# A new order for the first chunk of an encoder: transposes, roundings and loads of one graph kernel

## The chip, the cores and the metric

The kernel runs on one core of a Trainium2 chip. The metric is the time of one execution in microseconds of device time. The median of 3 runs of the kernel before is 487.85 us (485.99 to 488.41).

## The reference

Two graph layers stand one after the other, each on a layer norm with a relu and each with a residual. There are 1250 nodes with 1024 features, 20000 edges, and an inner width of 500. Cut to what matters:

```python
h = jnp.maximum(_layernorm(x), 0.0)
# first layer
e   = sigmoid(h @ wenc.T + benc)              # the encoder: 1250 x 1024 by 1024 x 500
agg = segment_sum((e @ conv_weight)[src] * edge_weight[:, None], dst)
x   = x + (agg + e @ lin_weight.T) @ wdec.T + bdec
# second layer
h   = jnp.maximum(_layernorm(x), 0.0)
x   = x + normalised_adjacency(src, dst) @ (h @ W.T + b)
```

The change touches only the start of the program: the layer norm and the encoder product of the first 250 nodes.

## The kernel before, in words

The nodes lie in 10 tiles of 125 rows, and two tiles make a chunk of 250 nodes; the encoder goes over five chunks. Every float32 product is computed in three parts from values that are split into a rounded high part and the low rest: high by high, high by low, low by high. So each operand needs a rounding ("high", a copy into the rounded type) and a difference ("low") before TensorE can use it.

For a tile `t` of the input the steps are:

- `load_x(t)`: a transfer of 512 KB from DRAM, issued by SyncE. Tiles 0 and 1 are loaded in two pieces of half rows.
- `stats t` (`row_stats`, L310 and L312): mean and variance on VectorE, in two halves of the row (`stats 1 0` is the first half alone) and an aggregate; then `factors` (L297 to L301), three small steps on GpSimd that turn them into scale and bias.
- `norm t` (`normed`, L273): the norm and relu in place on ScalarE, for the whole row or a half.
- `half t q` (`half_transposed`, L282 to L285): TensorE transposes four blocks of 128 columns into one PSUM buffer; a copy on ScalarE rounds them into `hnh` (L284; `halfv` has VectorE do it); VectorE writes the difference into `hnl` (L285).

The encoder's weights come in four transfers `wencf0` to `wencf3` of 500 KB. `high j` rounds one of them on ScalarE (L324, 128x1000), `highv j` on VectorE; `low k` writes the low part of half of one on VectorE (L330, 128x500), `lowp k` on GpSimd.

Chunk 0's product (L579) runs `k` over the eight blocks of 128 features. It keeps four PSUM accumulators, one for each 125 of the 500 outputs. For `k` = 0 the eight products that need only `hnh` come first, then the four that need `hnl`; `k` = 1 to 5 take twelve products each; the last two blocks go output by output, each followed by the sigmoid (L559). Chunk 1 and later chunks use the same products in another line (L347).

The order of all this is written out by hand: the table `ORDER` says which steps are recorded ahead of chunk 0's first product (slot `(0, -1)`) and after each block (`(0, 0)` after `k` = 0, and so on), and the recording order is the order of instructions on every engine until the encoder ends. Later stages are ordered by a scheduler. SyncE issues the loads in the order x0, x0, x1, x1, wencf0, wencf1, x2, wencf2, x3, wencf3, x4; from the ninth transfer on, an issue waits until the transfer eight places ahead of it has landed. Memory places come from a fixed plan. 18 products on zeroes (`warm`, L247) keep TensorE busy from the start until the first tile is there.

Of the kernel before, what the change touches and what calls it, by code (L numbers as in the profile page):

```python
# [41 lines left out]


ORDER = {
    (0, -1): "stats 0, stats 1 0, stats 1 1, norm 0 0, halfv 0 0, norm 0 1, high 0, low 0, lowp 1, "
             "highv 1, lowp 3, norm 1 0, norm 1 1, half 1 0, lowp 2, stats 2 0, stats 2 1, half 0 1, "
             "high 2, half 1 1, lowp 4",
    (0, 0): "stats 3 0, stats 3 1, lowp 5, stats 4, norm 2, high 3",
    (0, 3): "half 2 0, norm 3",
    (0, 4): "half 2 1",  # L50
    (0, 5): "low 7, lowp 6, stats 5, half 3 1, half 3 0",
    (0, 6): "norm 4",
    (0, 9): "stats 6",
    (1, 0): "norm 5",
    (1, 2): "half 5 0, stats 7, half 4 1",
# [81 lines left out]
def kernel(  # L137
# [16 lines left out]
    nc = tc.nc  # L154
# [3 lines left out]
    T = 125  # L158
# [22 lines left out]
    ps_t = ctx.enter_context(tc.tile_pool(name="ps_t", bufs=2, space=bass.MemoryType.PSUM))  # L181
    ps_oh = ctx.enter_context(tc.tile_pool(name="ps_oh", bufs=2, space=bass.MemoryType.PSUM))
# [9 lines left out]
    def move(dst_, src_, rest=nc.sync):  # L192

        n = dst_.shape[0]
        m = n - n % 16
        nc.sync.dma_start(dst_[:m], src_[:m])
        if m < n:
            rest.dma_start(dst_[m:], src_[m:])
# [6 lines left out]
    def rows(a, t):  # L205

        return a[: min(P, N - t * T)]

    def load_x(t):
        xs[t] = arena.tile([P, D], F32, f"x{t}")  # L210
        pieces = 2 if t < 2 else 1
        for i in range(pieces):
            cs = slice(i * D // pieces, (i + 1) * D // pieces)
            move(rows(xs[t], t)[:, cs], rows(x[t * T :, :], t)[:, cs])

    in_order = ExitStack()
    in_order.enter_context(tc.manual_schedule())
    load_x(0)
    load_x(1)
    wencf = [arena.tile([P, 2, EMB], F32, f"wencf{j}") for j in range(KD // 2)]  # L220
    for j, f in enumerate(wencf):
        nc.sync.dma_start(f, wenc_v[:, 2 * j : 2 * j + 2, :])
        if j > 0:
            load_x(j + 1)
    benc_sb = const.tile([T, EC], F32, name="benc_sb")
    nc.sync.dma_start(benc_sb, benc)
    dsb = const.tile([T, NS // T, GRAN], I32, name="dsb")
# [44 lines left out]
    def relu(to, xt, rs):  # L272
        nc.scalar.activation(to, xt, AF.Relu, bias=rs[:, 1:2], scale=rs[:, 0:1])  # L273

    def half_transposed(t, q, pool=ps_t, tag="pt", copy=nc.scalar.copy):

        hi, lo = hn[t // 2]
        at = slice(t % 2 * T, (t % 2 + 1) * T)
        p = pool.tile([P, 512], F32, tag=tag, name="pt")[:, : 4 * T].rearrange("p (k n) -> p k n", k=4)
        for k in range(4):  # L280
            kk = 4 * q + k
            nc.tensor.transpose(p[:, k, :], xs[t][:T, kk * P : (kk + 1) * P], ident[:T, :T])  # L282
        ks = slice(4 * q, 4 * q + 4)
        copy(hi[:, ks, at], p)  # L284
        nc.vector.tensor_sub(lo[:, ks, at], p, hi[:, ks, at])  # L285

    hn = {}

# [34 lines left out]
    def high_wenc(j, copy=nc.scalar.copy):  # L323
        copy(wenc[j][:, 0], wencf[j])  # L324
# [53 lines left out]
    def edge_rows():  # L378
        c = edges["below"]
        half = c.shape[1] // 2  # L380
        ps = ps_t.tile([P, 512], F32, tag="pt", name="pstart")
        for b in range(NB):
            for j in range(half):
                nc.tensor.matmul(
                    ps[:T, b : b + 1], c[:, j, b * T : (b + 1) * T], ones_b[:T],
                    start=(j == 0), stop=(j == half - 1),
                )
        arena.give("cmp0", "cmp1")
        sf = const.tile([T, NB], F32, name="sf")
        row = const.tile([T, NB], I32, name="row")  # L390
        nc.vector.tensor_scalar(sf, ps[:T, :NB], -1.0, 0.0, op0=OP.add, op1=OP.max)
        nc.vector.tensor_scalar(row, sf, float(NW - 1), None, op0=OP.min)
        edges["row"] = row
# [316 lines left out]
    parts = {}  # L710
    halves = []

    def half(t, q, copy=nc.scalar.copy):
        half_transposed(t, q, *((ps_oh, "poh") if t == 1 else (ps_t, "pt")), copy)
        halves.append(t)
        if halves.count(t) == 2:
            arena.give(f"x{t}")

    def split_lin():
        parts["lin"] = split_square("lin")  # L720

    what = {
        "stats": row_stats, "norm": normed, "half": half, "halfv": lambda t, q: half(t, q, nc.vector.tensor_copy), "load": load_x,
        "high": high_wenc, "highv": lambda j: high_wenc(j, nc.vector.tensor_copy),
        "low": low_wenc, "lowp": lambda k: low_wenc(k, nc.gpsimd),
        "starts": edge_starts, "rows": edge_rows, "gather": edge_gather, "fields": edge_fields,
# [107 lines left out]
    at = 0  # L834
# [17 lines left out]
    def decode(t, half):  # L852
        c, i = divmod(t, 2)
        ns = slice(i * T, (i + 1) * T)
        cs = slice(half * HALF, (half + 1) * HALF)
        p = ps_acc.tile([P, 512], F32, tag="acc", name="pdec")
        terms = []
        for k in range(EC):
            r = T + (k == 0)
            terms.append(  # L860
                (
                    [aggT[c][:r, s, k, ns] for s in range(2)],
                    [wdec[k][:r, s, cs] for s in range(2)],
                )
            )
        product(p[:T, :], terms)
        return p
# [220 lines left out]
    for i, t in enumerate(tiles):  # L1088
        st = small.tile([T, 2, 6], F32, name="st")
        for half in range(2):  # L1090
            slot = 2 * i + half
            p = decode(t, half)
# [541 lines left out]
```

## Time and profile before

| | |
|---|---|
| median of 3 runs | 487.85 us |
| the profiled execution | 487.37 us |
| its span, first to last instruction | 485.6 us |
| mean granted TensorE clock | 0.993 |
| TensorE busy | 474.9 us, 98% |
| VectorE, ScalarE, GpSimd busy | 336.0, 174.3, 81.5 us |
| first product of chunk 0 | 12.70 us |
| first product of chunk 1 | 26.58 us |

A profile is one execution. Its page gives the busy time of each engine, the span in 40 slices of 12.1 us, the transfers and the costliest groups; the timeline lists instructions in order of their start, with the idle time of the engine ahead of them and what ended it. PE is TensorE's matmul, PEld its weight load, DVE VectorE, ACT ScalarE, POOL GpSimd and SP SyncE. Times in the timeline are from the start of the span.

### The profile page before, as it was taken

Reading aid. Unit: us, or ns where it says so; the run is one execution under the profiler, and the core shown is the slowest. Engines: PE = TensorE matmul, PEld = TensorE weight load, DVE = VectorE, ACT = ScalarE, POOL = GpSimd, SP = SyncE. Lnnn points to the kernel's source line nnn. Section 1 sums busy time; section 2 is a strip of 40 time slices with the busy share of each in tenths; the row PEclk is TensorE's granted clock in tenths of the full one; section 3 lists DMA queues with packets and bytes.
Section 4 is the critical chain, followed back from the end, with each engine's and each line's share of the span. In section 5 each row is a group of like instructions: output and inputs, shape, how many; then the busy total and the mean of one; then the engine's idle time right before and its main releaser. Section 6 shows DMA issues by size and latency. Waiting matters only on the chain. (4 is left out here: it accounts for less than half of the span.)

```text
span 485.6 us, 9225 instructions
## 1 busy us (share of the span) xinstructions
PE 474.9 (98%) x3614; PEld 431.2 (89%) x3614; DVE 336.0 (69%) x763; ACT 174.3 (36%) x453; POOL 81.5 (17%) x134
## 2 busy tenths in 40 slices
PE   6999999999999999999999999999999999999995
PEld 3999999998889999999878889999998887788784
DVE  6777479977697958884457776968798554555541
ACT  4585543553433243451253345323265021110000
POOL 4734252410000010161123641000000000000000
PEclk9899999999999999999999999999999999999998
DMA  8993103000000204401999621022429064445441
GB/s 284 368 272 85 32 2 84 1 29 28 29 29 28 70 4 135 164 1 29 205 253 262 200 86 45 2 82 92 163 79 236 11 165 112 112 122 128 124 97 49
DMA packets 50899, 52.20 MB, mean 108 GB/s; under 512 B 29728, under 2 KB 39592, under 8 KB 50847
## 3 DMA queue, kind: packets, MB, share of 16 engines
q1 hardware_dynamic: 50449, 51.09, 37.2%
q8 instruction: 30, 0.49, 0.4%
q0 software_dynamic: 320, 0.39, 0.3%
q14 instruction: 22, 0.18, 0.1%
q10 hardware_dynamic: 78, 0.05, 0.0%
HBM read 34.61 MB, written 17.45 MB: 107 GB/s over the span
## 5 line engine op out<-in xcount | busy, mean ns | idle before, releaser
L1175 PE MATMUL pout<-w,zs 128*125 128x512 f32 (+1 forms) x336 | 100.8, 383 | 0.0
L347 PE MATMUL pagg<-A,h 125*125 125x250 f32 x600 | 74.7, 282 | 0.0
L1175 PEld LDWEIGHTS pout<-w,zs 128*125 128x125 f32 x336 | 61.3, 186 | 14.1
L347 PEld LDWEIGHTS pagg<-A,h 125*125 125x125 f32 x600 | 71.4, 187 | 0.1
L347 PE MATMUL pdec<-wdec,agg 126*125 126x512 f32 x240 | 56.2, 395 | 0.0
L347 PEld LDWEIGHTS pdec<-wdec,agg 126*125 126x125 f32 x240 | 44.7, 187 | 11.1
L1183 DVE SCALAR_TENSOR_TENSOR res<-pout,dinv,res 125x512 f32<-125x512 f32 (+1 forms) x21 | 15.2, 725 | 49.5 <-PE pout L1175 49.5
L952 PE MATMUL pz<-cts,y 125*128 125x312 f32 (+1 forms) x320 | 47.3, 307 | 0.2 <-DVE cts L818 0.2
L952 PEld LDWEIGHTS pz<-cts,y 125*128 125x128 f32 x320 | 46.4, 189 | 0.5 <-DVE cts L818 0.5
L523 ACT CAST A<-poh 125x100 fp32r<-125x100 f32 x150 | 25.5, 258 | 49.3 <-PE poh L513 49.3
L534 DVE TENSOR_TENSOR A<-poh,A 125x100 fp32r<-125x100 f32 x150 | 26.9, 234 | 13.3 <-ACT cnt L529 12.8
L952 PE MATMUL pz<-ct,y 125*128 125x312 f32 (+1 forms) x240 | 35.7, 307 | 0.0
L952 PEld LDWEIGHTS pz<-ct,y 125*128 125x128 f32 x240 | 35.0, 189 | 0.1
L347 PE MATMUL penc<-hnh,wenc 128*125 128x250 f32 x256 | 34.3, 283 | 0.0
L482 DVE TENSOR_TENSOR oh<-cols,eb 128x640 bf16<-128x640 bf16 x50 | 25.9, 522 | 8.5 <-PE poh L513 6.2
L347 PEld LDWEIGHTS penc<-hnh,wenc 128*125 128x125 f32 x256 | 31.3, 187 | 0.0
L347 PE MATMUL plin<-hT,lin 125*125 125x250 f32 x240 | 30.1, 282 | 0.0
L347 PEld LDWEIGHTS plin<-hT,lin 125*125 125x125 f32 x240 | 28.6, 187 | 0.0
L347 PE MATMUL pconv<-conv,hT 125*125 125x500 f32 x120 | 28.6, 392 | 0.0
L508 PE MATMUL poh<-oh 128*128 128x100 bf16 x250 | 28.1, 206 | 0.0
L512 PE MATMUL poh<-oh 128*128 128x50 bf16 x250 | 27.1, 187 | 0.0
L513 PE MATMUL poh<-oh 128*128 128x50 bf16 x250 | 27.0, 184 | 0.0
(180 smaller groups left out, 843.4 us busy)
## 6 DMA issues: line engine op xcount, KB each, us to landing
x<-in_x_dram SPq DMA_DIRECT2D x14, 512.0 KB
x_d<-x SPq DMA_DIRECT2D x9, 512.0 KB
res<-x_d SPq DMA_DIRECT2D x9, 512.0 KB
out_dram<-res SPq DMA_DIRECT2D x19, 224.0 KB
c_d<-cnt SPq DMA_DIRECT2D x10, 320.0 KB
cr<-c_d SPq DMA_DIRECT2D x10, 312.5 KB
x<-in_x_dram SPq DMA_DIRECT2D x8, 256.0 KB
wencf<-in_wencT_dram SPq DMA_DIRECT2D x4, 500.0 KB
```

The costliest lines, as they stand in the source:

```text
L347: nc.tensor.matmul(p, left[i], right[j], start=(part == 0 and n == 0), stop=(part == 2 and n == len(terms) - 1),)
L482: nc.vector.tensor_tensor(pairs(bo), pairs(cols).unsqueeze(1).to_broadcast([P, PB, P // 2, 2]), eb[:, gs].unsqueeze(2).to_broadcast([P, PB ...
L508: nc.tensor.matmul(p[:, g, :], left, mv[:, g, 0:2, :].rearrange("p q m -> p (q m)"), start=True, stop=False,)
L512: nc.tensor.matmul(p[:, g, M:], left, mv[:, g, 2, :], start=False, stop=False)
L513: nc.tensor.matmul(p[:, g, M:], left, mv[:, g, 3, :], start=False, stop=True)
L523: nc.scalar.copy(hi, whole)
L534: nc.vector.tensor_sub(lo, whole, hi)
L952: nc.tensor.matmul(p, left[m, which][:, s, j, :], right[:, j, c0:c1], start=(first and j == 0 and s == 0), stop=(last and j == NP - 1 and ...
L1175: nc.tensor.matmul(acc[u][:T, : cs.stop - cs.start], zs[t][:, i, half, m, :], w1[k][j][:, cs], start=(m == 0 and half == 0 and n == 0), st ...
L1183: nc.vector.scalar_tensor_tensor(x1[t][:, cs], acc[u][:T, : cs.stop - cs.start], dinv[:, t : t + 1], x1[t][:, cs], op0=OP.mult, op1=OP.add,)
```

## The change

The order of chunk 0 is written anew, and `half` is split into its three steps, so that they can be ordered apart: `turn t q` (the transposes), `hi t q` (the rounding, on ScalarE) and `lo t q` (the difference, on VectorE). In the new table tile 0's second half is transposed ahead of tile 1's first; tile 1's second half is transposed after the products of `k` = 0. VectorE rounds the first weights, ScalarE rounds all transposed tiles, and VectorE takes the low parts 0, 2, 5 and 7 (0 and 7 before), GpSimd 1, 3, 4 and 6. Tile 2's statistics follow the split of tile 1's first half; statistics and norms of tiles 2 to 4 move to other slots. Tile 1 is loaded by one transfer of whole rows, and `wencf3` ahead of tile 3. Tile 1 is loaded once more, in a later stage, by one transfer too.

```diff
 ORDER = {
-    (0, -1): "stats 0, stats 1 0, stats 1 1, norm 0 0, halfv 0 0, norm 0 1, high 0, low 0, lowp 1, "
-             "highv 1, lowp 3, norm 1 0, norm 1 1, half 1 0, lowp 2, stats 2 0, stats 2 1, half 0 1, "
-             "high 2, half 1 1, lowp 4",
-    (0, 0): "stats 3 0, stats 3 1, lowp 5, stats 4, norm 2, high 3",
-    (0, 3): "half 2 0, norm 3",
-    (0, 4): "half 2 1",
-    (0, 5): "low 7, lowp 6, stats 5, half 3 1, half 3 0",
-    (0, 6): "norm 4",
+    (0, -1): "stats 0, stats 1 0, stats 1 1, norm 0 0, turn 0 0, norm 0 1, hi 0 0, turn 0 1, highv 0, "
+             "low 0, lowp 1, lo 0 0, norm 1 0, turn 1 0, hi 1 0, lo 1 0, norm 1 1, highv 1, lowp 3, "
+             "low 2, hi 0 1, lo 0 1, high 2, lowp 4, stats 2 0, stats 2 1",
+    (0, 0): "turn 1 1, hi 1 1, high 3, lo 1 1, low 5, norm 2, lowp 6, stats 3, low 7",
+    (0, 3): "stats 4",
+    (0, 4): "half 2 0, norm 3",
+    (0, 5): "half 2 1",
+    (0, 6): "half 3 1, half 3 0, stats 5, norm 4",
...
-        pieces = 2 if t < 2 else 1
+        pieces = 2 if t == 0 else 1
...
-        if j > 0:
-            load_x(j + 1)
+        if j == 1:
+            load_x(2)
+    for t in (3, 4):
+        load_x(t)
...
-    def half_transposed(t, q, pool=ps_t, tag="pt", copy=nc.scalar.copy):
+    turned = {}
+    def turn(t, q):
+        pool, tag = (ps_oh, "poh") if t in (1, 3) else (ps_t, "pt")
         p = pool.tile([P, 512], F32, tag=tag, name="pt")[:, : 4 * T].rearrange("p (k n) -> p k n", k=4)
         for k in range(4):
             kk = 4 * q + k
             nc.tensor.transpose(p[:, k, :], xs[t][:T, kk * P : (kk + 1) * P], ident[:T, :T])
         ks = slice(4 * q, 4 * q + 4)
-        copy(hi[:, ks, at], p)
-        nc.vector.tensor_sub(lo[:, ks, at], p, hi[:, ks, at])
+        turned[t, q] = [p] + [h[:, ks, t % 2 * T : (t % 2 + 1) * T] for h in hn[t // 2]]
+    def turned_high(t, q):
+        p, hi, lo = turned[t, q]
+        nc.scalar.copy(hi, p)
+    def turned_low(t, q):
+        p, hi, lo = turned[t, q]
+        nc.vector.tensor_sub(lo, p, hi)
...
+    def half(t, q):
+        turn_half(t, q)
+        turned_high(t, q)
+        turned_low(t, q)
```

Tile 3's transposes now use the PSUM buffers that only tile 1's used before.

## The prediction

> **What bounds the kernel now.** First the page: its sections 1 and 2 say which engine sets the end and where it isn't full.
>
> ```profile
> span 485.6 us, 9225 instructions
> PE 474.9 (98%) x3614; PEld 431.2 (89%) x3614; DVE 336.0 (69%) x763; ACT 174.3 (36%) x453; POOL 81.5 (17%) x134
> PE   6999999999999999999999999999999999999995
> PEclk9899999999999999999999999999999999999998
> ```
>
> TensorE is busy in every slice but the first and last, so a microsecond won on it early is a microsecond won at the end, if nothing else is late. Next, TensorE's waits, which say where it stood still.
>
> ```profile
> PE pt L282 <- ACT x L273: 3.2, 2, 2.4
> PE warm L247 <- DVE idle L244: 1.2, 1, 1.2
> PE pz L952 <- DVE cts L818: 0.2, 1, 0.2
> ```
>
> Two waits of 0.85 and 2.4 us for a normed tile: all that an order of the first chunk can win by waiting less. Then the windows, cut where the clock changes (columns: length, busy time and count of PE, PEld, DVE, ACT, POOL, then clock, DMA share, GB/s).
>
> ```profile
> 4.51:7.92 3.41, 2.56 (x13) 1.07 (x12) 2.55 (x6) 1.05 (x2) 1.07 (x4) 1.00 0.93 296
> 7.92:11.34 3.42, 1.02 (x9) 0.79 (x9) 2.66 (x4) 2.83 (x4) 2.31 (x4) 1.00 1.03 405
> 11.34:14.75 3.41, 3.41 (x19) 3.41 (x18) 3.38 (x6) 2.75 (x5) 2.79 (x3) 0.50 1.03 407
> 14.75:18.16 3.41, 3.41 (x31) 3.41 (x31) 3.32 (x7) 1.89 (x2) 2.97 (x7) 1.00 1.03 397
> ```
>
> After a stretch with TensorE busy 30% of the time the clock is 0.50 for 3.41 us; that is a second cost, and an order can save it. Last the timeline, for the chain that ends at the first product.
>
> ```profile
> 3.95 1.30 DVE L310 BATCH_NORM_STATS2 st<-x 125x6 f32<-125x512 f32 x2 [1.74 <-DMA x<-in_x_dram]
> 5.29 0.21 DVE L312 BATCH_NORM_AGGREGATE mv<-st 125x2 f32<-125x12 f32 x1
> 6.57 0.27 POOL L301 TENSOR_SCALAR rs<-mv,rs 125x1 f32<-125x1 f32 x1
> 6.89 0.69 DVE L310 BATCH_NORM_STATS2 st<-x 125x6 f32<-125x512 f32 x1 [0.50 <-DMA x<-in_x_dram]
> 8.98 1.02 ACT L324 CAST wenc<-wencf 128x1000 fp32r<-128x1000 f32 x1 [0.59 <-DMA wencf<-in_wencT_dram]
> 9.91 1.52 ACT L273 ACTIVATE x<-x,rs 125x512 f32<-125x512 f32 x2
> 10.04 0.68 DVE L330 TENSOR_TENSOR wenc<-wencf,wenc 128x500 fp32r<-128x500 f32 x1 [0.23 <-ACT wenc L324]
> 10.09 1.74 POOL L330 TENSOR_TENSOR wenc<-wencf,wenc 128x500 fp32r<-128x500 f32 x1 [0.93 <-ACT wenc L324]
> 10.63 1.74 DVE L324 CAST wenc<-wencf 128x1000 fp32r<-128x1000 f32 x1
> 10.78 2.26 PE L282 MATMUL pt<-ident,x 125*128 125x125 f32 x12 [2.40 <-ACT x L273]
> 11.46 0.58 ACT L284 CAST hnh<-pt 128x500 fp32r<-128x500 f32 x1
> 12.70 2.02 PE L579 MATMUL penc<-hnh,wenc 128*125 128x250 f32 x8
> ```
>
> ScalarE stood 0.59 us for the first weights and took 1.02 to round them before it normed tile 1 (9.91); then came 12 transposes in a row, and the products start at 12.63 (weight load; matmul record 12.70). Chunk 1 starts at 26.58, and from there the order on every engine is nearly the old one, so the effect is the shift of that 26.58.
>
> **The change, part by part.** *TensorE's own work* is only moved: 32 transposes in 8 groups of four and 96 products lie before chunk 1 in both. At full clock the trace steps 0.118 us per product (60 of them and two groups, 15.10 to 22.92), a group of four costs 0.355 more, the pair of groups in a row 0.775. Half clock steps 0.208. New: one group (tile 1's second half) now stands behind the first 12 products instead of ahead of them. So from the first product at S, all warm, chunk 1 starts at S + 96 x 0.118 + 3 x 0.355 + 0.775 = S + 13.17, plus 0.433 us for each microsecond spent at half clock (1 - 0.118/0.208). Before, the same sum with two groups from 12.83 (the first product's true slot, after the last transpose) gives 26.5 where 26.58 stands.
>
> *S after the change.* Tile 1 now comes in one transfer of whole rows, so its first statistics can't start at 5.70 on the first half. Bytes ahead of its end are the same, so I put its landing where the second half landed, 6.87. Bounds: 5.7, where the first half landed, and 8.96, where the next transfer landed (ScalarE's wait ended at 8.98). Both halves' statistics then follow: 1.55 us (3.95 to 5.50), to 8.44, against 7.83 before: 0.6 later. POOL's three factors, 5.50 to 6.84, take 1.34: 9.78. ScalarE is free by then (tile 0's second half ends at 8.4, its new rounding of tile 0 at 9.0), since the weights' rounding is DVE's now, and norms half a tile; from there to the transposes are 0.87 us (9.91 to 10.78): 10.68. Transposes to rounding, 0.68 (10.78 to 11.46): 11.36. Rounding 0.58 and the handover 0.07: S = 12.0. TensorE starts 0.6 us earlier, not 2.4.
>
> *What hides the rest.* ScalarE gives DVE the rounding of the first weights and gets tile 0's first rounding for it (0.58); POOL gives DVE two of its six low parts (1.26 to 1.74 there, 0.68 on DVE). DVE takes the first weights' rounding: 1.74 from 8.98, to 10.72; low part 0.68, to 11.40, when the first product still waits; two differences of 0.68, to 12.76, needed after eight products (13.7 at half clock, 12.95 at full). Second weights 1.74 and low part 0.68: 15.2; needed at 14.5 + 0.5 + 1.4 = 16.4 at half clock, 15.2 at full. Then a difference of 0.68 and statistics of 1.55, to 17.4; POOL is at its third low part until 17.9 (15.2 - 0.68 + 2 x 1.74), its factors take 1.34 and the norm 1.24: tile 2 is normed at 20.5 at most. Its transposes, moved back one slot, come at S + 12 products + group + 48 products: 20.7 at half clock, 19.4 at full: hidden in the first, up to 1.1 us of stall in the second. If the casts take less, the stall goes to nothing; I take none at half clock. Tile 3's norm has a slack of half a microsecond on the same terms. *SyncE* issues one transfer fewer (about 0.47 us each), which gains nothing because the queues are full (371 to 413 GB/s from 6.9 on): a transfer of 500 KB takes 1.3 us whoever issues it. Fourth weights before tile 3 cost tile 3 those 1.3 us; it lands near 15.5 and is read after 18. Tile 1's reload in a later stage is one transfer instead of two, where DMA is idle most of the time.
>
> *The clock.* The stretch 7.92 to 11.34 will hold three groups of transposes, 0.46 + 0.65 + 0.65 = 1.76 us, 51%. The rows bracket that: 30% was followed by half clock, 75% was not. It is a hair nearer 30%, and in kind it is like that row, which held transposes alone, while the 75% held warming products. I take half clock again, to 14.75: S + 13.17 + 0.433 x 2.75 = 26.36, a gain of 0.2 us. At full clock it would be 25.17, a gain of 1.4.
>
> The Trainium skill, "TensorE: Matmul & The Clock Gate", Part 4: PE-mode transpose, says that transposes do not count as TensorE's activity as products do: by it the third group buys no clock, and the sum is the gain of 0.2. Its practical table, in the same page, warns only of idle gaps of some 3 us; the 2.40 us gap here was followed by half clock all the same, so that figure doesn't hold for this trace, and by it the sum would be the gain of 1.4.
>
> *The shared cast.* The DVE cast ran from 10.63 to 12.37 while POOL's subtraction ran to 11.83. Alone it may take from 0.54 (what is left after 11.83) to 1.74; I take 1.74, the row itself, for what DVE owes, and it is hidden. Ahead of it, though, POOL's factors of tile 1 run 8.44 to 9.78, just when it starts; if it holds POOL up by 0.54, S is 12.5 and the gain becomes a loss of 0.1. The Trainium skill, "SBUF — State Buffer", calls the port pair of DVE and GpSimd an exclusive lock held for a whole instruction by such copies: by it that loss is the sum, a rule that speaks against putting this cast on DVE here.
>
> **The rivals.** (a) Full clock: three groups are enough activity. For it: 51% is well over 30%. Against: transposes alone. Price: gain 1.4, less up to 1.1 of stall on tile 2: 486.4 to 487.5. (b) Tile 1 lands early as whole rows: 1.3 us, the later rate, after tile 0's second half, which landed at 4.54 by the transfer records, is 5.85; S, 5.1 later, is 11.0, and with full clock chunk 1 starts at 24.15, gain 2.4: 485.4. For it: half-tile transfers landed 1.2 us apart at the start, where 0.65 would do at the later rate. Against: bytes and queues are the same. (c) Slower: tile 1 lands late. All statistics now wait for all its rows; if they drain together with the first weights at 8.96, S is 14.1 and chunk 1 starts at 14.1 + 13.17 + 0.3 = 27.55, a loss of 1.0: 488.8. It decides from a landing of 7.25 (S = 12.39, where the half-clock sum equals 26.58). For it: transfers overlap in the 16 queues. Against: landings came in order in the trace.
>
> **How the numbers follow.** The profiled execution took 487.37 us (span 485.6 and 1.8 around it), 0.48 under the median 487.85; a shift is added to either alike. Forecast, half clock again: 487.85 - 0.2 = 487.6, chance 0.5. (a) 0.22, (b) 0.08, (c) 0.2. The runs before lie between 485.99 and 488.41, so a median of a few may be off by a microsecond: range 485.6 to 489.1, from below (a) to just past (c). A measurement of this kernel tells about 0.5%, 2.4 us, from no change. Faster by more needs (b) and a low draw, or an unforeseen gain: 0.11. Slower by more needs (c) with a stall behind it: 0.12. Within: 0.77.
>
> **What would show it.** Right: TensorE's wait of 2.4 us becomes some 1.6 and 0.7; the first product near 12.0; ScalarE norms tile 1 near 9.8 without the wait for weights; clock 0.50 in one stretch; chunk 1 near 26.4. Wrong: a clock of 1.00 throughout (a), tile 1's statistics starting before 6.3 (b) or after 7.25 (c), or a wait of TensorE for tile 2's or 3's norm.

## The result, and the profile after

The changed kernel took 490.58 us (median of 9 runs, 488.05 to 491.83) where the kernel before took 486.86 us beside it (9 runs): a ratio of 1.0065, with a 95% interval of 1.005 to 1.008. By this ratio it is 3.2 us slower (the medians lie 3.7 us apart). Measured again later, it took 488.94 us against 486.42, 1.0052 (1.0036 to 1.0068), 2.5 us slower. The forecast was 487.6 us, a gain of 0.2 us, with a range of 485.6 to 489.1. The first time lies above the range; the second lies inside it, with a loss and not the gain.

The page of the changed kernel, sections 1 and 2. TensorE's busy time is 1.5 us longer, its count the same: the same work, some of it at a slower clock. Most of it costs nothing: the 18 products on zeroes at the start ran until 8.12 us instead of 6.88, because the clock first rose at 7.01 instead of 4.51, and after them TensorE waits for tile 1 all the same.

```profile
span 488.1 us, 9225 instructions
PE 476.4 (98%) x3614; PEld 431.5 (88%) x3614; DVE 336.0 (69%) x765; ACT 173.9 (36%) x453; POOL 79.8 (16%) x132
```

TensorE's waits in the changed kernel. No wait for tile 2 or tile 3 is among them, and the one for tile 1 has grown from 2.4 to 3.6 us, with 0.7 more for its rounding.

```profile
PE pt L285 <- ACT x L275: 3.6, 1, 3.6
PE penc L589 <- ACT hnh L291: 0.7, 1, 0.7
```

The windows of the changed kernel, cut where its clock changes (columns as before). The stretch of waiting holds 19% of TensorE's time, and the half clock after it (PEclk 0.50) now lies mostly on products: twelve of them and one group of transposes, where before it also held most of the 12 transposes of the start.

```profile
7.01:10.42 3.41, 2.11 (x13) 1.20 (x11) 2.15 (x5) 1.99 (x3) 0.54 (x1) 1.00 1.02 378
10.42:13.83 3.41, 0.65 (x4) 0.41 (x4) 1.15 (x2) 1.27 (x2) 2.45 (x3) 1.00 1.03 410
13.83:17.25 3.42, 3.24 (x15) 3.24 (x16) 3.23 (x6) 2.23 (x4) 1.92 (x2) 0.50 1.00 393
```

The timeline of the changed kernel, the chain to the first product.

```profile
8.20 1.29 DVE L320 BATCH_NORM_STATS2 st<-x 125x6 f32<-125x512 f32 x2 [2.67 <-DMA x<-in_x_dram]
9.52 0.21 DVE L322 BATCH_NORM_AGGREGATE mv<-st 125x2 f32<-125x12 f32 x1
9.64 0.63 DVE L334 CAST wenc<-wencf 128x1000 fp32r<-128x1000 f32 x1
9.81 0.54 POOL L307 TENSOR_SCALAR ve<-mv 125x1 f32<-125x1 f32 x1 [2.95 <-DVE mv L322]
10.31 0.68 DVE L340 TENSOR_TENSOR wenc<-wencf,wenc 128x500 fp32r<-128x500 f32 x1
10.44 0.99 POOL L308 TENSOR_TENSOR rs<-ve,half_neg 125x1 f32<-125x1 f32 x1
11.82 0.81 ACT L275 ACTIVATE x<-x,rs 125x512 f32<-125x512 f32 x1 [2.66 <-POOL rs L311]
12.69 0.65 PE L285 MATMUL pt<-ident,x 125*128 125x125 f32 x4 [3.58 <-ACT x L275]
14.01 0.57 PE L589 MATMUL penc<-hnh,wenc 128*125 128x250 f32 x1 [0.67 <-ACT hnh L291]
```

DVE waited 2.67 us for all of tile 1, which landed at 8.18 by the transfer records, not at 6.87. Then GpSimd's first step took 0.54 us where it takes 0.22, and its second 0.99 where it takes 0.57: each ended 0.1 to 0.5 us after VectorE was through with the cast (10.27) or the low part (10.98). The first product came at 14.01 instead of 12.70. Chunk 1 started at 28.86 instead of 26.58:

```profile
28.86 0.39 PE L357 MATMUL penc<-hnh,wenc 128*125 128x250 f32 x2
```

So 2.28 of the 2.5 us between the two spans are lost in the first chunk. The other 0.2 come up in one step near 109 us, between two products that write `poh`; their cause is open. In a second profile of the changed kernel, shown under after_again, chunk 1 started at 29.06, and all of the difference to the kernel before (2.48 us) stands there already.

### The profile page after: what moved, and what is told of

Read it like the earlier page. It is cut to its first block, busy times and chain, and to the rows that moved or that the text cites. A ratio compares the mean times of both kernels' runs of the same rounds, so it can differ in the third digit from the quotient of the medians.

```text
span 488.1 us, 9225 instructions
## 1 busy us (share of the span) xinstructions
PE 476.4 (98%) x3614; PEld 431.5 (88%) x3614; DVE 336.0 (69%) x765; ACT 173.9 (36%) x453; POOL 79.8 (16%) x132
```

## The experiments

Three theories. A: tile 1 lands late as one whole-row transfer, and all its statistics wait for it. B: the new order costs by itself, through VectorE's queue or through the cast beside GpSimd's factors. C, formed after the first four: the half clock behind TensorE's wait is what the first chunk pays most for, and the new order pays it for longer. "Half clock" stands for a granted clock of 0.50; the products then step 0.208 us instead of 0.118.

**order_only**, the new order with the old transfers:

```diff
-        pieces = 2 if t == 0 else 1
+        pieces = 2 if t < 2 else 1
...
-        if j == 1:
-            load_x(2)
-    for t in (3, 4):
-        load_x(t)
+        if j > 0:
+            load_x(j + 1)
```

> The new order with all transfers as before (tile 1 in two half-row transfers, the fourth weights behind tile 3). Theory A, tile 1's single whole-row transfer lands late and that is most of the loss: here its second half lands near 6.9, the aggregate is done at 7.8, the factors by 9.2 to 9.7, the first product is at 11.4 to 11.9 and chunk 1 at 26.0 to 26.4: 0.2 to 0.6 us faster than before (486.3 to 486.7 where before is 486.9). Theory B, the new order itself costs (DVE's queue, the cast against GpSimd): 1.5 to 3 us slower than before, like the changed kernel.

Measured: 488.05 us, ratio 1.0024 (1.0007 to 1.004), so 1.2 us slower. The chain went as theory A said (aggregate done at 7.72, first product at 11.92, 0.8 earlier than before), and yet chunk 1 started at 27.88. The windows say why: the stretch at half clock did not end after 3.41 us.

```profile
10.81:14.23 3.42, 2.75 (x14) 2.37 (x13) 2.30 (x5) 2.68 (x4) 1.51 (x2) 0.50 1.05 412
14.23:17.64 3.41, 3.41 (x18) 3.41 (x18) 3.00 (x7) 1.50 (x2) 3.14 (x5) 0.50 1.03 397
```

The first of the two holds the 0.67 us wait between tile 1's transposes and the first product: 80% busy. Before, that stretch was full, because 12 transposes stood in a row ahead of the products.

**loads_only**, the old order with the new transfers (the same lines of the loads, changed in the kernel before).

> The old order with the new transfers (tile 1 whole, the fourth weights ahead of tile 3). Theory A: tile 1 lands near 8.2, its aggregate is done at 9.7, factors at 11.1 without any hold-up, norm to 12.0, then 12 transposes: first product at 13.5 to 14.0 and 1 to 2 us slower than before. Theory B: within 0.3 us of before.

Measured: 487.9 us, ratio 1.0026 (1.0011 to 1.0041), 1.3 us slower, as theory A said. But the profiled execution of it had a span of 485.3 us, below the kernel before, with tile 1 at 7.57, the first product at 12.68 (before: 12.70) and chunk 1 at 25.76: its clock never fell in the first chunk.

```profile
6.30:9.71 3.41, 1.90 (x11) 0.92 (x9) 2.04 (x5) 2.35 (x3) 0.68 (x3) 1.00 1.01 367
9.71:13.12 3.41, 1.76 (x15) 1.71 (x16) 3.38 (x4) 2.79 (x6) 2.69 (x4) 1.00 1.03 405
```

Its wait of 3.2 us happened to lie across two stretches, 56% and 52% busy. In this execution the later tile 1 cost the first product nothing: it came 3.55 us after tile 1's aggregate, where the kernel before took 4.87, with ScalarE's rounding of the first weights in between. So the 1.3 us are not explained by this profile. Here GpSimd's steps, with no cast beside them, took 1.25 us:

```profile
9.21 0.22 POOL L299 TENSOR_SCALAR ve<-mv 125x1 f32<-125x1 f32 x1 [2.58 <-DVE mv L314]
9.52 0.58 POOL L300 TENSOR_TENSOR rs<-ve,half_neg 125x1 f32<-125x1 f32 x1
10.20 0.27 POOL L303 TENSOR_SCALAR rs<-mv,rs 125x1 f32<-125x1 f32 x1
```

**high_on_act**, the changed kernel with ScalarE rounding the first weights:

```diff
-"... hi 0 0, turn 0 1, highv 0, low 0, lowp 1, lo 0 0, norm 1 0, turn 1 0, ..."
+"... hi 0 0, turn 0 1, high 0, lo 0 0, low 0, lowp 1, norm 1 0, turn 1 0, ..."
```

> The changed kernel with the first weights rounded by ScalarE instead of VectorE, and the first low part behind tile 0's first difference. Theory B's second half, that VectorE's cast and low part hold GpSimd's factors up by 0.7 us: GpSimd's three steps take 1.35 to 1.6 us instead of 2.06, the first product comes at 13.3 to 13.6 instead of 14.0, 0.3 to 0.6 us faster than the changed kernel. Rival, GpSimd is slow for another reason: 2.06 us again, and the time of the changed kernel.

Measured: 489.77 us, ratio 1.007 (1.0056 to 1.0083). GpSimd's steps took 1.58 us (the low part still met the last one), as expected of the lock, and the first product came at 12.94; but the time is that of the changed kernel and not the 0.3 to 0.6 us less that were expected. Its profile had 6.83 us at half clock, as order_only's had, the first stretch 80% busy. For the time this run decides nothing.

**halves**, the changed kernel with only `pieces` set back.

> The changed kernel with tile 1 in two half-row transfers again; the fourth weights stay ahead of tile 3. Theory A: like the kernel with the new order alone, 0.2 to 0.6 us faster than before. If the place of the fourth weights and of tile 3 cost anything, this one is slower than that kernel by it; I expect under 0.2 us.

Measured: 487.96 us, ratio 1.0012 (0.9992 to 1.0033): beside order_only's 488.05 the place of the fourth weights costs nothing that can be seen. Both missed the expected gain. Its times are wide apart, 484.84 to 489.69 us; the profile had one stretch at half clock.

Then the clock was held up. Products on zeroes fill TensorE's wait; nothing reads them.

```diff
+    def fill(n):
+        for _ in range(n):
+            nc.tensor.matmul(warm, idle[:, :P], idle, start=True, stop=True)
...
-"... norm 0 0, halfv 0 0, norm 0 1, ..."             (kernel before)
+"... norm 0 0, halfv 0 0, fill 10, norm 0 1, ..."    (before_fill)
-"... norm 1 0, turn 1 0, hi 1 0, ..."                (new order)
+"... norm 1 0, fill 8, turn 1 0, fill 2, hi 1 0, ..."  (order_fill; after_fill has 12 and 2)
```

**before_fill.**

> The kernel before, with ten more products on zeroes (0.213 us each) behind tile 0's first transposes, where TensorE waits 2.4 us for tile 1's norm. Theory C, the half clock behind that wait is what the first chunk pays most for: no stretch at 0.50 before the tail, chunk 1 at 25.0 to 25.8, 1 to 2 us faster than before. Rival, the clock does not follow the activity of products on zeroes, or the products delay tile 1's transposes: within 0.3 us of before, or slower.

Measured: 486.17 us, ratio 0.9986 (0.9974 to 0.9998), and 12 runs within 485.77 to 486.66. No half clock before the tail, chunk 1 at 25.01. The stretch that holds the wait is now full:

```profile
9.25:12.66 3.41, 3.41 (x26) 2.70 (x25) 3.41 (x5) 3.03 (x6) 2.02 (x3) 1.00 1.03 410
```

The gain is 0.7 us over many runs, less than the 1.6 of the one profile.

**order_fill.**

> The new order with the transfers as before, eight products on zeroes ahead of tile 1's first transposes and two behind them. It was 1.2 us slower than before without them, though its first product came 0.7 us earlier; its profile had half clock for 6.8 us. Theory C: no half clock, chunk 1 at S + 13.2 = 25.0 to 25.4, 1 to 1.8 us faster than before. Rival, the order's queues cost the 1.2 us: still slower than before.

Measured: 486.88 us, ratio 0.9992 (0.9978 to 1.0005). The 1.2 us loss of order_only is gone, but the expected gain isn't there: in this profile GpSimd's steps took 1.78 us beside the cast and the first product came at 12.67.

**after_fill.**

> The changed kernel with twelve products on zeroes ahead of tile 1's first transposes and two behind them. Theory C with theory A: no half clock, but the first product still at 13 to 14, so chunk 1 at 26.2 to 27.2: 2.5 to 3.5 us faster than the changed kernel and within 0.6 us of before. If the lateness of tile 1 alone were the loss, it would stay 2 us or more slower than before.

Measured: 487.88 us, ratio 1.002 (1.0005 to 1.0035). Of the changed kernel's loss of 2.5 to 3.2 us against the kernel before, 1.0 is left. That does not yet make the clock the larger part, because the kernel before gains 0.7 us from a held clock itself. Tile 1 landed at 8.08, GpSimd took 1.98 us, the first product came at 13.90 and chunk 1 at 27.33 with the clock at 1.00.

**best**, order_fill with the cast behind tile 0's first difference (`... turn 0 1, lo 0 0, highv 0, low 0, lowp 1, norm 1 0, ...`).

> The new order with the transfers as before, the first weights' cast behind tile 0's first difference on VectorE so that GpSimd's factors are through, and the products on zeroes (eight and two). GpSimd's three steps take 1.25 to 1.4 us instead of 1.75 to 2.0, first product at 11.3 to 11.6, chunk 1 at 24.5 to 24.9: 1.5 to 2.3 us faster than before, and 0.3 to 0.6 us faster than the same without the cast moved.

Measured: 486.18 us, ratio 0.9988 (0.9975 to 1.0001), and a missed expectation: the aggregate was done at 8.27, late enough that the cast at 9.04 met the factors all the same (2.20 us), and the first product came at 12.77.

**whole_fill**, before_fill with tile 1 in one transfer (`pieces = 2 if t == 0 else 1`), and **rows_fill**, before_fill with tile 1 in two transfers of 64 whole rows:

```diff
+            if t == 1:
+                rr = slice(i * P // 2, (i + 1) * P // 2)
+                move(rows(xs[t], t)[rr], rows(x[t * T :, :], t)[rr])
+            else:
...
```

> The kernel before with the ten products on zeroes, and tile 1 in one whole-row transfer, nothing else of the change. Theory A by itself, with the clock held at 1.00: tile 1 lands near 7.7 instead of 7.0, its statistics all follow it, the aggregate is done near 9.3 instead of 8.0, and the time is 1.0 to 1.5 us above that of the same kernel with two half-row transfers (486.2): 487.2 to 487.7. Rival, the transfer is hidden behind the weights' rounding on ScalarE: under 0.3 us.

> The same, but tile 1 in two transfers of 64 whole rows each. It splits theory A: the statistics wait for all of the tile again (0.6 us), but the transfers are half as large. If the late landing comes with one transfer of 512 KB, tile 1 lands near 7.0 and the time is 0.5 to 0.7 us above two half-row transfers; if it comes with rows of 4 KB, it lands near 7.7 and the time is that of the kernel with one transfer.

Measured: whole_fill 486.5 us, 1.0001 (0.9992 to 1.0011); rows_fill 486.83 us, 1.0007 (0.9998 to 1.0017). Against before_fill's 0.9986 that is 0.7 and 1.0 us (medians: 0.3 and 0.7), each uncertain by some 0.7 us by the two intervals, so the loss of one transfer alone is not clear of noise. Theory A had said 1.0 to 1.5 us for it, its rival under 0.3; the 0.7 lies between. The runs do not split as meant: in these profiles the single transfer landed at 6.22 and the two at 6.83. Over six profiles with one transfer tile 1 landed at 6.22 to 8.18 (mean 7.46); over seven with half rows the second half landed at 6.75 to 7.63 (mean 7.18). In the mean the landing is 0.3 later, and it swings by 2 us. What all these profiles show is the wait of both halves' statistics for all of the tile: the aggregate is done 1.55 us after the landing, against 0.96.

**act_late**, the new order with the old transfers, ScalarE rounding the first weights between tile 1's norm and its rounding, and products on zeroes:

```diff
-"... turn 0 1, highv 0, low 0, lowp 1, lo 0 0, norm 1 0, turn 1 0, hi 1 0, ..."
+"... turn 0 1, lo 0 0, norm 1 0, fill 8, turn 1 0, fill 4, high 0, hi 1 0, low 0, lowp 1, ..."
```

> The new order with the transfers as before, eight and four products on zeroes, and the first weights rounded by ScalarE between tile 1's norm and its first rounding, so that neither the cast nor the first low part meets GpSimd's factors. If they held those up by 0.5 to 0.9 us: GpSimd's three steps take 1.25 us, the first product is at 11.6 to 12.0, 0.4 to 0.9 us faster than the same order with the cast on VectorE (486.9): 486.0 to 486.5. If GpSimd is slow for another reason, the time stays at 486.9 or more.

Measured: 486.18 us, ratio 0.9992 (0.998 to 1.0004). GpSimd took 1.26 us and the first product came 3.63 us after the aggregate, against 4.08 in order_fill: the hold-up is shown in the trace. In the time it isn't: the median is where it was expected, but the ratio to the kernel before is order_fill's.

**after_again**, the changed kernel once more.

> The changed kernel itself once more, for another place of the clock's 3.41 us stretches. Tile 1 in one transfer has landed between 6.2 and 8.2 in five profiles; GpSimd's three steps take 1.9 to 2.0 us again, because the cast meets them. Theory C as the profiles so far have it: the clock falls after a stretch with TensorE busy 42% or less and comes back only after one with 95% or more. So there is one stretch at half clock where the first one is nearly full, as in the first profile, and two (6.83 us) where the first products start more than 0.7 us after it begins. A rival in which the half clock lasts one stretch always would show 3.41 us in both.

Measured: the second ratio above. Its profile had the half clock for 6.83 us, as the rule for the first product's place said (13.47, 1.97 us into the stretch):

```profile
8.09:11.50 3.41, 0.39 (x4) 0.16 (x2) 2.43 (x5) 0.96 (x2) 2.48 (x4) 1.00 1.03 406
11.50:14.91 3.41, 2.53 (x11) 2.14 (x12) 1.42 (x3) 2.22 (x5) 0.62 (x2) 0.50 1.05 408
14.91:18.33 3.42, 3.42 (x18) 3.42 (x18) 3.01 (x6) 1.72 (x3) 3.25 (x4) 0.50 1.02 403
```

GpSimd took 1.98 us again, with tile 1 landed at 7.19. The span was 488.0 us, as in the first profile, by another sum: product earlier, half clock longer.

Put together in ratios, times 486.7 us: with the clock held up in both, the changed kernel loses 1.65 us to before_fill (1.002 against 0.9986; uncertain by some 0.9 us). That is what the later first product costs. How it splits is not shown: the whole-row transfer alone makes 0.7 and the order alone 0.3, each no larger than its uncertainty. The clock adds 1.6 to 2.2 us to the changed kernel and 0.7 to the kernel before, so it makes 0.9 to 1.5 us of the difference.

The mean granted clock of every execution, profiled or not, supports theory C. The profiles with half clock in the first chunk have means of 0.991 to 0.994, those without it 0.996 to 0.999. Counted by this (the kernel before: the executions beside the experiments):

| kernel | executions | of them at 0.995 or less | median of these, us | median of the others, us |
|---|---|---|---|---|
| before | 100 | 36 | 487.4 | 486.2 |
| loads_only | 12 | 7 | 488.2 | 486.5 |
| halves | 12 | 7 | 488.3 | 485.6 |
| order_only | 12 | 10 | 488.2 | 486.0 |
| high_on_act | 6 | 6 | 489.8 | none |
| changed | 15 | 15 | 489.8 | none |
| the seven with products on zeroes | 81 | 0 | none | 486.2 to 487.9, by kernel |

By this count the kernel before pays the half clock in about a third of its executions and the changed kernel in all of them, and the products on zeroes take it away. The execution of the kernel before that was profiled at first was one of the third.

## Why the prediction was wrong, point by point

- **S = 12.0, the term that failed most.** The first product came at 14.01 and 13.47 in the two profiles of the changed kernel, and that is 2.0 and 1.5 of the 2.5 and 2.7 us by which chunk 1 missed its 26.36. With the measured landing and GpSimd's steps the prediction's own chain gives 8.18 + 5.13 + 0.7 = 14.0 in the first. In the second it gives 7.19 + 5.13 + 0.7 = 13.0; the rest is that tile 1's transposes took 1.10 us instead of 0.65, at half clock. So two terms of S were mis-sized, and the other steps were right.
- **Landing at 6.87.** It was 8.18 and 7.19. The upper bound 8.96 held. Over all profiles the landing swings too much to be taken from one row.
- **POOL's factors at 1.34.** The three steps took 1.98 us in both profiles, where they take 1.25 in the rows before. The prediction had the mechanism and priced it at 0.54, as a gain turned into a loss of 0.1, but left it out of the sum. Two instructions of VectorE meet the factors, the cast and the low part, so it was 0.7. The exclusive lock that the Trainium skill describes ("SBUF — State Buffer", "Who interferes with whom") agrees with these rows; the row without overlap was the wrong choice.
- **The cast at 1.74 on DVE.** It took 0.63: the row of before was mostly a wait for POOL, whose subtraction ended at 11.83. The error was harmless, and tile 2 was never waited for.
- **The clock: one stretch, 11.34 to 14.75.** That half clock would come was right; its place was not, and its length only in one of two profiles. The stretches lay at 13.83 to 17.25 in the first profile and at 11.50 to 18.33 in the second, so their end can't be taken from another execution. With S = 14.01 and the first of these the prediction's own formula gives 14.01 + 13.17 + 0.433 x 3.24 = 28.58, against 28.86. In the second profile 4.86 us of the products lay at half clock and not 2.75, which is 0.9 us more; the formula gives 28.74 against 29.06, so 0.3 us stay open in both. A stretch at half clock that was 74 to 80% busy was followed by another in all three profiles that had one, 3.41 x 0.433 = 1.5 us more. That splitting the 12 transposes from the products makes this likelier is argued, not shown. The prediction asked only whether the stretch ahead would be busy enough, and never whether the first one at half clock would be full. It also took the half clock for a fixed cost of the kernel before, where 64 of 100 executions don't have it.
- **Transposes and the clock.** The Trainium skill ("TensorE: Matmul & The Clock Gate", Part 4) says that transposes do not count as products do. For the clock's fall the traces speak against counting them at nothing. The second stretch of loads_only was 52% busy, 13% of it with products and the rest with transposes, and the clock stayed at 1.00. At the end of before_fill a stretch with products alone, 34% busy, was followed by half clock from 480.29 on. How much a transpose counts stays open. The first line is loads_only's, with the products into `penc` alone, the second before_fill's:

```profile
9.71:13.12 3.41, 0.44 (x3) 0.44 (x4) 0.00 (x0) 1.00 1.03 405
476.87:480.29 3.42, 1.16 (x10) 0.96 (x9) 0.48 (x1) 0.00 (x0) 0.00 (x0) 1.00 0.22 64
```

- **Right:** TensorE's work is only moved (3614 matmuls in both), no gain from SyncE's saved issue shows, the fourth weights' place costs nothing that can be seen, and what is lost before chunk 1 is lost at the end.
- **Rivals.** (a) did not come true in the changed kernel, whose waiting stretch was 19% or 12% busy and not 51%, since tile 1 came later. (b) did not come true. (c) stood on the right side: it named the wait of all statistics for all rows. Its S of 14.1 is near the measured 14.01 by luck, since it put the landing 0.8 us too late and left out the lock (0.7 us); its price of 1.0 us also left out most of a stretch at half clock.

## What to carry to other kernels

TensorE's clock should be read by what stands in each stretch of 3.41 us and not by the waits alone: a wait was paid twice here where the work behind it then ran at half clock, and the half clock ended after a full stretch of work but not after one with gaps. One profile does not tell how often a kernel pays this; the mean clock of many executions tells more, and by it the kernel before paid in 36 of 100. Dummy products in a wait that can't be removed cost nothing that can be seen where the engine would stand still (before_fill 486.17 us, the executions of the kernel before without half clock 486.2), and they made the times steadier: 485.77 to 486.66 over 12 runs, against 485.43 to 488.46 over 35 of the kernel before beside them. Before a step is moved onto VectorE, look at what GpSimd is doing at that moment: a 0.6 us cast and a 0.7 us subtraction held up two tiny steps of GpSimd, for which the whole start waits, by 0.3 and 0.4 us.

## What the runs showed of the hardware that was not expected

- In these traces the clock of TensorE changes only at edges 3.41 us apart, and the edges lie differently in each execution: it first rose at 4.51, 7.01, 3.99, 6.30 and 5.38 us in five of them. That the windows run free is also what the Trainium skill says ("TensorE: Matmul & The Clock Gate", Part 1). Whether half clock comes goes with much of the spread of the kernels without dummy products (the table above).
- In the first chunk the clock fell after stretches with TensorE 12, 19, 23, 25, 30 and 41% busy and stayed after 52, 56 and 58%. From half clock it came back after stretches 95 to 100% busy, and did not after 74, 80 and 80% (at the very start, on warming products alone, it once rose after 81%).
- A single transfer of 512 KB early in the program finished on 15 of the 16 transfer engines by 6.20 us and on the last at 8.18 in one execution (the first profile of the changed kernel), and on all by 6.22 in another (whole_fill). In the first, the next two transfers show the same lag: 15 engines by 7.47 us and the last at 9.47, then 8.91 and 10.78. Its cause is open.
- A weights' cast of 128x1000 on VectorE took 0.63 to 0.68 us where no large subtraction of GpSimd was already running, and 1.74 in the kernel before, where one was.
